# A graph network in two parts on one core: another order of the node blocks in the second part, and two pairs of steps swapped

## The chip, the cores and the metric

The kernel runs on one core of one Trainium2 chip. The metric is the device time of one execution, in microseconds (us). Every run gives one such time; what is compared is the median of several runs.

## The reference

There are 6250 nodes with 64 features each and 200,000 directed edges, sorted by their destination. A first network (one attention layer with a gate) and a normalisation come first. Then comes the second network, in which the change lies: three layers of attention over the edges with eight heads, each followed by a gate and a small two-layer network. `dst` and `src` are an edge's destination and source node, `edge_attr` is the same in all three layers.

```python
edge_attr = _mlp(_ln(edge_embed, eng, enb), eW1, eb1, eW2, eb2)
for l in range(L):                                   # L = 3
    h = _ln(x, n1g[l], n1b[l])
    xi, xj = (h[dst], h[src])
    q = (xi @ Wq[l] + bq[l]).reshape(-1, H, HD)      # H = 8 heads of HD = 8
    kn, vn = ...                                     # xj @ Wkn[l], xj @ Wvn[l]
    ke, ve = ...                                     # edge_attr @ Wke[l], edge_attr @ Wve[l]
    alpha = (q * (kn + ke)).sum(-1) / scale
    amax = jax.ops.segment_max(alpha, dst, num_segments=n)
    ex = jnp.exp(alpha - amax[dst])
    den = jax.ops.segment_sum(ex, dst, num_segments=n)
    alpha = ex / (den[dst] + 1e-16)
    msg = ((vn + ve) * alpha[..., None]).reshape(-1, D)
    agg = jax.ops.segment_sum(msg, dst, num_segments=n)
    gate = jax.nn.sigmoid(agg @ Wih[l] + bih[l] + h @ Whh[l] + bhh[l])
    upd = agg + gate * (h @ Wself[l] + bself[l] - agg)
    x = x + upd @ Wout[l] + bout[l]
    h2 = _ln(x, n2g[l], n2b[l])
    x = x + _mlp(h2, mW1[l], mb1[l], mW2[l], mb2[l])
```

## The kernel before

**Blocks.** The nodes are sorted by their number of edges and cut into 49 blocks of 128, one node to a partition. Block 0 holds the nodes with the most edges, block 48 those with the fewest. A block has SL[b] columns: column k holds the k-th edge of each of its nodes, so that a block's attention is a softmax along a row of columns. The first NW = 20 columns ("o") hold only edges with sources in certain blocks: column k those from blocks k, k + 20 and k + 40. The rest hold the other edges: the "a" columns have a gathered row each, and the "z" columns use such a row a second time. SL goes from 56 for block 0 down to 32 for block 48.

**Where the source rows come from.** At the end of a layer (or of the first network) each node's key and value products are stored in DRAM as a row of a table (`tab`), split into three bfloat16 parts. There are two such tables, for even and odd layers. A layer reads its table in two ways. First, the whole table is copied once into SBUF (`ftb`, seven copies of seven blocks, `refill`, L1274); the "o" columns take their rows from it by multiplying with 0/1 matrices `ohl`, which are loaded for each block (L1246). Second, for the other columns POOL issues indirect DMAs, one for each "gather" of 128 rows (L1254): NT[b] of them for block b, from 30 for block 0 to 7 for block 48, 859 in all. Gathers of a block are cut into chunks of at most CL = 12 (`cuts`); a chunk fills one buffer of the tile `g1`, and there are four such buffers (the pool `l_g`). The first four chunks are asked for when a layer starts (`start`); after that, using up a chunk asks for the one that is four further on in the order of blocks (`gather`, called in the main loop). The chunks of block 0 are 10, 10, 10, those of block 1 are 10, 10, 7, of blocks 2 and 3 they are 10, 10, 5, of block 4 12 and 12; blocks with 13 to 24 gathers have two chunks and those with up to 12 have one.

**A block's life.** The loop of L1479 counts i, and in iteration i block b = LORDER[i] has its columns summed, while the blocks b1, b2, b3 and b4 of the four iterations before it go through their later stages. In program order an iteration does the following.

- The softmax of b1 (`soft`), the norm of b3's new x (`updated`), and the weighted sum over b1's values (`values`), all on VectorE with the exponential on ScalarE; then the small loads of the next block (`begin`).
- The query of b (L1504). Then, group of columns by group of columns, `sums`: TensorE adds into a PSUM tile `b_pk` the products of the edge features (L1324), and either the rows picked from `ftb` (L1344) or the gathered rows (L1331); ScalarE copies keys and values out of it (L1348). After a part of the columns VectorE makes the scores (`scores`, L1355 and L1356). `b_pk` has two buffers.
- Between the groups six steps are called, spread evenly over them (the list `steps`, L1512 to L1515). They hold the work of b2, b3 and b4.

The functions that the steps call are these:

- `turned`: b2's weighted sum `b_ag` is transposed on TensorE (L571, in the helper `flip`) and copied out by ScalarE (L574).
- `gate` and `gated`: three products on TensorE (L1405 to L1407), a tanh on ScalarE (L1409), and four VectorE operations (from L1414 on).
- `update`: b2's output product; `updated`, in the next iteration, adds it to x (L1425) and normalises.
- `turned2`: b3's normalised x, `b_h2`, is transposed in the same helper (L571) and copied out with scale and shift (L576). The profile writes names without their last digits, so it shows as `b_h`.
- `hidden` and `close`: the small network of b3 (L1436, L1443 to L1445), the sum into x (L1446), the store of x, and the start of `prepare`, which makes the next layer's table row: a norm, a transposition (L601), a product (L613) with copies, and further parts of the split. b4 takes these parts one at a time through `then` and `more`.

**What sets the order.** The code of this network is under a manual schedule: each engine runs its instructions in program order. SyncE's queue carries the loads of edge features, of the 0/1 matrices, the small loads and the stores; POOL's queue carries the gathers, and in the last layer the output rows. The transpositions and the products of `gate`, `update`, `hidden`, `close` and `prepare` share the PSUM tile `p_pm`, which has two buffers (the pool `l_m`). After the 49 blocks a layer has four more iterations in which no block is summed; in them the steps of the last blocks run back to back.

**The order of blocks.** Before, it was

```python
48, 47, 1, 46, 0, 45, 2, 44, 3, 43, 4, 42, 5, 41, ..., 21, 25, 22, 24, 23
```

Block 48 has to come before block 0: the last block has unused rows that carry a part of the edges of block 0's nodes, and `values` joins them there.

Of the kernel before, what the change touches and what calls it, by code (L numbers as in the profile page):

```python
# [47 lines left out]
LB = NB - 1  # L48
# [1 line left out]
SPARE = P - LN  # L50
ORDER = (1, LB, 0) + tuple(range(2, LB))

LORDER = (LB, LB - 1) + tuple(b for i in range(24) for b in ((1, 0, *range(2, 24))[i], LB - 2 - i)) [:-1]
CAPE = tuple(c + c % 2 for c in CAPS)
FIRST = tuple(sum(CAPS[:b]) for b in range(NB + 1))
SLOTS = FIRST[NB]
# [54 lines left out]
def cuts(c, last=False, most=CH):  # L111

    if last:
        k = (c - 6) // 2 * 2
        return [(0, k), (k, c)]
    n = -(-c // most)
    w = 2 * -(-c // (2 * n))
    return [(k, min(k + w, c)) for k in range(0, c, w)]
# [3 lines left out]
def gnn_resnorm(ctx: ExitStack, tc: tile.TileContext, ins: dict, out: bass.AP):  # L122
# [33 lines left out]
    with tc.tile_pool(name="hd", bufs=1) as hd, tc.tile_pool(name="hd2", bufs=2) as hd2, \  # L156
# [271 lines left out]
        nc.vector.tensor_scalar(flag, vio[:, 2:3], 0.0, None, ALU.not_equal)  # L428

    passes(tc, ins, out, meta_d, t0_d, own_d, ident, row_f, ones, norm_c, st_i, id_i, off, end, has, hash_, rdeg, flag)  # L430
    away = nc.values_load(flag[0:1, 0:1], min_val=0, max_val=1)
    with tc.If(away > 0):
# [4 lines left out]
def passes(ctx, tc, ins, out, meta_d, t0_d, own_d, ident, row_f, ones, norm_c, st_i, id_i, off, end, has, hash_, rdeg,  # L437
# [143 lines left out]
    def flush():  # L581
        while stores:
            stores.pop(0)()
# [49 lines left out]
    with tc.tile_pool(name="e_g", bufs=4) as gp, tc.tile_pool(name="e_x", bufs=2) as xp, \  # L633
# [475 lines left out]
        for i in range(NB + 4):  # L1109
# [46 lines left out]
            for s in range(STEPS):  # L1156

                b = bs[3]
# [48 lines left out]
    with tc.tile_pool(name="l1", bufs=1) as fp, tc.tile_pool(name="l_g", bufs=4) as gp, \  # L1207
# [8 lines left out]
        todo = {}  # L1216
        for b in LORDER:
            tn, lc = NT[b], LCAPS[b]
            todo[b] = [(b, 0, 12, "o", 0), (b, 12, NW, "o", 0)]
            for t0, t1 in cuts(tn, b == LORDER[-1], CL):  # L1220
                todo[b].append((b, NW + t0, NW + t1, "a", t0))
                o0, o1 = max(tn, 2 * tn - t1), min(lc, 2 * tn - t0)
                if o0 < o1:
                    todo[b].append((b, NW + o0, NW + o1, "z", t0))
        loads = [(l, *t[:3]) for l in range(3) for b in LORDER for t in todo[b]]
        gathers = [(b, t0, t1) for b in LORDER for t0, t1 in cuts(NT[b], b == LORDER[-1], CL)]
        ohq = [(l, b, w0) for l in range(3) for b in LORDER for w0 in list(range(0, NW, 4)) + [NW]]
        eas, gs, ohs, ms, wanted_ = {}, {}, {}, {}, []

        def load():  # L1230
            if loads:
                l, b, k0, k1 = loads.pop(0)
                e0, e1 = k0 // 2, (k1 + 1) // 2
                eas[l, b, k0] = ep.tile([P, 8, P], F32, name="eal")
                nc.sync.dma_start(eas[l, b, k0][:, : e1 - e0, :], ea_d[b][:, e0:e1, :])

        def load_oh():
            if ohq:
                l, b, w0 = ohq.pop(0)
                if w0 == NW:  # L1240
                    oh = ohs[l, b, w0] = op.tile([P, 2, P], BF, name="oh2", bufs=3)
                    nc.sync.dma_start(oh, oh_d[b][:, NU * P :].rearrange("p (u n) -> p u n", n=P))
                    return
                n, u0 = 4 * most(w0), unit(w0, 0)
                oh = ohs[l, b, w0] = op.tile([P, 12, P], BF, name="ohl")
                nc.sync.dma_start(oh[:, :n, :], oh_d[b][:, u0 * P : (u0 + n) * P].rearrange("p (u n) -> p u n", n=P))  # L1246

        def gather(l):
            if wanted_:
                b, t0, t1 = wanted_.pop(0)  # L1250
                g = gs[l, b, t0] = gp.tile([P, CL, WT], F32, name="g1")
                for t in range(t0, t1):
                    f = TFIRST[b] + t
                    nc.gpsimd.indirect_dma_start(  # L1254
                        out=g[:, t - t0, :], out_offset=None, in_=tabs[l % 2][:],
                        in_offset=bass.IndirectOffsetOnAxis(ap=idx[:, f : f + 1], axis=0))

        def begin(l, b):
            hv = wk.tile([D + 1, P], F32, name="hv", bufs=5)
            nc.sync.dma_start(hv, ht_d[l % 2][b][:])  # L1260
            xb = wk.tile([P, D], F32, name="b_x", bufs=6)
            nc.sync.dma_start(xb, (x1_d if l == 0 else x2_d)[b][:])
            xv = None
            if l == 2:
                xv = wk.tile([P, D], F32, name="xv", bufs=6)
                nc.sync.dma_start(xv, x1_d[b][:])
            ms[b] = dict(hv=hv, xb=xb, xv=xv)
# [13 lines left out]

        begin(0, LORDER[0])
        for _ in range(5):
# [7 lines left out]
        i = 0  # L1291
        while i < NB:
# [4 lines left out]
            i = j  # L1297
# [15 lines left out]
        for l in range(3):  # L1313
# [39 lines left out]
            def scores(m, k0, k1):  # L1353
                k = m["k"][:, : k1 - k0]
                nc.vector.tensor_tensor(k, k, m["q"].unsqueeze(1).to_broadcast([P, k1 - k0, D]), ALU.mult)  # L1355
                nc.vector.tensor_reduce(m["al"][:, :, k0:k1].rearrange("p h k -> p k h"), k.rearrange("p k (h d) -> p k h d", h=H),  # L1356
                                        AX.X, ALU.add)
# [113 lines left out]
            def put():  # L1471
                while last:
                    b, n, y = last.pop(0)
                    nc.gpsimd.indirect_dma_start(
                        out=out[:], out_offset=bass.IndirectOffsetOnAxis(ap=id_i[:n, b : b + 1], axis=0),
                        in_=y[:n, 1, :], in_offset=None)

            last = []
            for i in range(NB + 4):  # L1479
                b, b1, b2, b3, b4 = [LORDER[i - k] if 0 <= i - k < NB else None for k in range(5)]  # L1480

                def do(b, *fs):
                    if b is not None:
                        for f in fs:
                            f(b, ms[b])

                do(b1, soft)
                do(b3, updated)
                do(b1, values)
                if i + 1 < NB:  # L1490
                    begin(l, LORDER[i + 1])
                elif i == NB and l < 2:
                    begin(l + 1, LORDER[0])
                if l < 2 and i == 1:
                    fresh = weights(l + 1)
                    nxt = next(fresh)
                if l < 2 and i == 2:
                    next(fresh, None)
                groups = []
                if b is not None:  # L1500
                    m, c = ms[b], SL[b]
                    qe = aps.tile([P, 512], F32, name="b_qe")
                    m["q"], m["ex"] = qe[:, :D], qe[:, D : D + c * H].rearrange("p (h k) -> p h k", h=H)
                    nc.tensor.matmul(m["q"], m["hv"], w["wc"][:, :D], start=True, stop=True)  # L1504
                    m["al"] = wk.tile([P, H, c], F32, name="b_al")
                    m["v"] = wk.tile([P, D, MS], F32, name="b_v")
                    for part in todo[b]:
                        k0, k1 = part[1:3]
                        n = -(-(k1 - k0) // 8)
                        n = 2 * -(-(k1 - k0) // (2 * n))  # L1510
                        groups += [(part, u, min(u + n, k1)) for u in range(k0, k1, n)]
                steps = [lambda: (do(b4, then), do(b2, turned)),  # L1512
                         lambda: (do(b3, turned2), do(b2, gate, gated)), lambda: do(b4, more, then),
                         lambda: (do(b3, hidden), do(b4, more)), lambda: (do(b3, close), do(b4, then)),
                         lambda: (do(b2, update), do(b4, more))]  # L1515
                done = 0
                for j, (part, u0, u1) in enumerate(groups):
                    k0, k1, kind = part[1:4]
                    if u0 == k0:
                        m["k"] = wk.tile([P, 16, D], F32, name="b_k", bufs=3)  # L1520
                    sums(m, part, u0, u1)
                    if u1 == k1:
                        scores(m, k0, k1)
                        load()

                        if kind != "o" and (j + 1 == len(groups) or groups[j + 1][0][4] != part[4]):
                            gather(l)
                    if kind == "o":
                        load_oh()
                        if u1 == k1:  # L1530
                            load_oh()
                        if u1 == NW:
                            load_oh()
                    while done < len(steps) and done < len(steps) * (j + 1) // len(groups):
                        steps[done]()
                        done += 1
                for f in steps[done:]:
                    f()
                flush()
                put()  # L1540
                if b4 is not None:
                    stored.add(b4)
                if l < 2 and b is None:
                    refill(l + 1, stored, left)
# [695 lines left out]
```

## Time and profile before

Five runs took 10798.19 to 10823.06 us, with a median of 10804.39. The profiled execution took 10803.97 us, and its span, from the first recorded instruction to the last, is 10802.2 us.

| stretch of the span | us | PE busy | DVE busy | ACT busy | POOL busy | PE clock |
|---|---|---|---|---|---|---|
| up to the second network, 0 to 4798.6 | 4798.6 | 2511.4 | 2402.7 | 1463.4 | 1725.9 | 0.71 |
| first layer, 4798.6 to 6764.2 | 1965.6 | 1442.8 | 1043.0 | 534.7 | 795.0 | 0.78 |
| second layer, 6764.2 to 8754.6 | 1990.4 | 1458.7 | 1043.8 | 535.3 | 829.4 | 0.77 |
| third layer and the end, 8754.6 to 10802.2 | 2047.6 | 1448.9 | 1164.2 | 498.2 | 877.1 | 0.76 |
| whole span | 10802.2 | 6861.8 | 5653.6 | 3031.6 | 4227.4 | 0.74 |

PE is TensorE, DVE is VectorE, ACT is ScalarE, POOL is GpSimd and SP is SyncE; PEld is the loading of weights into TensorE. Busy means that an instruction's own time lies there; issuing a DMA from SyncE is not counted, while an indirect DMA on POOL is. The PE clock is the share of full speed that was granted. A row of the profile's groups reads: line, engine, operation, output tile and input tiles, number of instructions, then after the bar the busy time and the mean of one in ns, then the idle time of the engine just ahead of them and what ended most of it. A row of the timeline reads: start, duration, engine, line, operation, number of instructions, and in brackets the idle time before it with what released it; "issue" means that the engine waited for nothing that the profile can show.

In a layer TensorE has the most busy time of the four engines, some 1450 of 1966 to 2048 us. Its two largest groups in the second network are the picking of rows from `ftb` (L1344, 1930.1 us in three layers) and the products of the edge features (L1324, 1414.0 us).

### The profile page before, as it was taken

The numbers are of one execution on the slowest core, as the hardware profiler recorded it, in microseconds if no ns is written. First come the engines' busy times: TensorE is split into PE (matmuls) and PEld (weight loads), VectorE is DVE, ScalarE is ACT, GpSimd is POOL, SyncE is SP. The second block draws the span as 40 slices with busy tenths as digits, with TensorE's granted clock in tenths as the row PEclk, the third lists the DMA queues.
The fourth block names the chain that finished last, engine by engine and source line by source line (L and its number), as shares of the span: only waits on it lengthen the run. The fifth ranks groups of instructions, "written<-read, shape, count | busy, mean of one in ns | idle before, by whom it ended". The sixth has DMA issues, their size and how long they took to land.

```text
span 10802.2 us, 162686 instructions
## 1 busy us (share of the span) xinstructions
PE 6861.8 (64%) x61936; PEld 4733.5 (44%) x61936; DVE 5653.6 (52%) x14987; ACT 3031.6 (28%) x6298; POOL 4227.4 (39%) x4450
## 2 busy tenths in 40 slices
PE   2535455555555555666777777567777766777776
PEld 1212222222222223335556666456566645665665
DVE  5535455544445555534555555355555544656556
ACT  1323233322333333332222223222222222222222
POOL 5343433333333333324444443444444434444443
PEclk6667777766766677777777777777777777777777
DMA  4333333333333333344444444444444444444443
GB/s 101 98 89 93 99 98 98 90 94 95 95 89 92 91 92 89 95 110 130 131 126 133 134 134 133 123 126 131 131 135 132 132 127 114 128 127 124 130 129 92
DMA packets 1089117, 1218.64 MB, mean 113 GB/s; under 512 B 654756, under 2 KB 810041, under 8 KB 1081295
## 3 DMA queue, kind: packets, MB, share of 16 engines
q1 hardware_dynamic: 626639, 719.43, 22.6%
q0 software_dynamic: 186576, 417.85, 15.3%
q10 hardware_dynamic: 275120, 70.87, 3.2%
q8 instruction: 498, 8.16, 0.3%
q14 instruction: 284, 2.33, 0.1%
HBM read 968.74 MB, written 238.86 MB: 112 GB/s over the span
## 4 chain that ended last, share of the span: by engine, by line
PE 53%; another core or an unknown queue 19%; issue 18%; ACT 5%; DVE 3%; DMA 1%; POOL 0%; SPq 0%; ACTq 0%; POOLq 0%; DVEq 0%
PE b_pk L1344 18%; PE b_pk L1324 12%; PE f_ph L996 6%; PE b_pk L1331 4%; PE f_tr L959 4%; PE f_pe L978 3%; ACT f_hid L1000 1%; ACT f_sq L759 1%; ACT ea L982 1%; PE p_pm L1436 1%; ACT s_bc L841 1%; PE p_pm L838 1%; PE p_pm L1445 1%; ACT f_xt L963 1%
## 5 line engine op out<-in xcount | busy, mean ns | idle before, releaser
L1254 POOL DMA_INDIRECT g<-tab,fidx x2577 | 2487.2, 965 | 3546.9 <-PE b_pk L1331 1721.6
L740 POOL DMA_INDIRECT g<-ft_d,si x1596 | 1522.9, 954 | 2795.1 <-PE e_pt L1059 2322.5
L1344 PE MATMUL b_pk<-ftb,ohl 128*128 128x128 bf16 x21609 | 1930.1, 262 | 732.3 <-issue 684.0
L1344 PEld LDWEIGHTS <-ohl 128*128 128x128 bf16 x21609 | 1715.9, 121 | 971.4 <-issue 929.1
L1324 PE MATMUL b_pk<-fwkv,eal 64*128 64x128 f32 x12240 | 1414.0, 315 | 710.5 <-issue 660.1
L1355 DVE TENSOR_TENSOR b_k<-b_k,b_qe 128x768 f32<-128x768 f32 (+8 forms) x729 | 519.9, 713 | 2425.4 <-ACT b_k L1348 1834.7
L1324 PEld LDWEIGHTS b_pk<-fwkv,eal 64*128 64x128 f32 x12240 | 1038.5, 203 | 990.4 <-issue 881.7
L1348 ACT COPY b_k<-b_pk 128x384 f32<-128x384 f32 (+2 forms) x927 | 445.5, 481 | 3547.0 <-remote 1462.4
L978 PE MATMUL f_pe<-f_hid,fw 128*64 128x448 f32 (+4 forms) x2400 | 754.2, 650 | 1071.2 <-issue 716.8
L996 PE MATMUL f_ph<-f_xt,fw 64*128 64x448 f32 (+4 forms) x2400 | 821.4, 700 | 555.1 <-ACT f_xt L963 482.3
L963 ACT ACTIVATE f_xt<-f_tr,feg 128x336 f32<-128x336 f32 (+11 forms) x392 | 247.3, 631 | 2253.2 <-remote 1891.2
L978 PEld LDWEIGHTS f_pe<-f_hid,fw 128*64 128x64 f32 x2400 | 153.0, 152 | 1541.2 <-issue 1049.8
L1348 ACT COPY b_v<-b_pk 128x384 f32<-128x384 f32 (+2 forms) x927 | 822.5, 887 | 0.0
L1000 ACT ACTIVATE f_hid<-f_ph,fb 128x448 f32<-128x448 f32 (+4 forms) x1200 | 694.6, 624 | 448.1 <-PE f_ph L996 303.8
L959 PE MATMUL f_tr<-f_mv,f_xs 128*64 128x42 f32 (+11 forms) x12544 | 577.9, 255 | 346.7 <-issue 344.1
L946 DVE TENSOR_TENSOR f_mv<-s_tt,e_fac 128x672 f32<-128x672 f32 (+11 forms) x392 | 333.4, 851 | 874.7 <-remote 718.8
L959 PEld LDWEIGHTS f_tr<-f_mv,f_xs 128*64 128x64 f32 x12544 | 528.9, 167 | 456.4 <-issue 430.2
L996 PEld LDWEIGHTS f_ph<-f_xt,fw 64*128 64x128 f32 x2400 | 267.4, 223 | 912.6 <-ACT f_xt L963 614.7
L1356 DVE TENSOR_REDUCE b_al<-b_k 128x96 f32<-128x768 f32 (+8 forms) x729 | 520.7, 714 | 25.1
L1331 PE MATMUL b_pk<-g,oh 128*128 128x384 bf16 (+2 forms) x2682 | 496.8, 321 | 0.0
L1375 DVE TENSOR_REDUCE b_ag<-b_v 128x64 f32<-128x2560 f32 (+19 forms) x147 | 430.5, 2928 | 5.1
L1374 DVE TENSOR_TENSOR b_v<-b_v,b_qe 128x2560 f32<-128x2560 f32 (+19 forms) x147 | 429.1, 2919 | 0.0
(405 smaller groups left out, 7649.7 us busy)
## 6 DMA issues: line engine op xcount, KB each, us to landing
ohl<-oh_d SPq DMA_DIRECT2D x441, 384.0 KB
ohl<-oh_d SPq DMA_DIRECT2D x294, 256.0 KB
eal<-ea_d SPq DMA_DIRECT2D x189, 384.0 KB
eal<-ea_d SPq DMA_DIRECT2D x249, 256.0 KB
oh_d<-s_oh SPq DMA_DIRECT2D x147, 384.0 KB
g<-tab,fidx POOLq DMA_INDIRECT x2577
eal<-ea_d SPq DMA_DIRECT2D x117, 320.0 KB
ea_d<-ea ACTq DMA_DIRECT2D x154, 224.0 KB
```

The costliest lines, as they stand in the source:

```text
L740: nc.gpsimd.indirect_dma_start(out=g[:, k - k0, :], out_offset=None, in_=t0_d[:], in_offset=bass.IndirectOffsetOnAxis(ap=got[b]["si"][:, k ...
L959: nc.tensor.matmul(pv[r * D : (r + 1) * D, j], xss[(4 * ORDER.index(b) + 4 * j0 // D) % 4][:, (j0 + j) % (D // 4), :], mv[:, j, :, r::2], ...
L978: nc.tensor.matmul(pe[h * D : (h + 1) * D, :w], w2[:, s, :], hid[s][:, h, :w], start=(s == 0), stop=(s == 1))
L996: nc.tensor.matmul(ph[h][:, :w], w1[r, s * P : (s + 1) * P], xf[r, e0 * D : e1 * D], start=True, stop=True)
L1000: nc.scalar.activation(hid[s][:, h, :w], ph[h][:, :w], AF.Relu, bias=b1[:, s : s + 1])
L1254: nc.gpsimd.indirect_dma_start(out=g[:, t - t0, :], out_offset=None, in_=tabs[l % 2][:], in_offset=bass.IndirectOffsetOnAxis(ap=idx[:, f : ...
L1324: nc.tensor.matmul(pk[:, j % 2, j // 2, :], ea[r, e, :], w["wkv"][r], start=(j < 2), stop=False)
L1331: nc.tensor.matmul(pk[:, h, :c, :], ohs[l, b, NW][:, 0, :], rows_[:, slice(t, t + 2 * c - 1, 2), i, :], start=False, stop=(i == 2))
L1344: nc.tensor.matmul(pk[:, h, j, :], o, rows[:, i, :], start=False, stop=(j == c - 1 and q == len(us) - 1 and i == 2))
L1348: nc.scalar.copy(to.rearrange("p (j h) d -> p h j d", h=2), pk[:, :, : n // 2, d0 : d0 + D])
L1355: nc.vector.tensor_tensor(k, k, m["q"].unsqueeze(1).to_broadcast([P, k1 - k0, D]), ALU.mult)
L1356: nc.vector.tensor_reduce(m["al"][:, :, k0:k1].rearrange("p h k -> p k h"), k.rearrange("p k (h d) -> p k h d", h=H), AX.X, ALU.add)
```

## The change

Two things change, in the constants and in the main loop of the second network. No function is added, and the six steps hold the same calls.

```diff
-LORDER = (LB, LB - 1) + tuple(b for i in range(24) for b in ((1, 0, *range(2, 24))[i], LB - 2 - i)) [:-1]
+LORDER = (LB, LB - 1, LB - 2, LB - 3) + tuple(b for i in range(23) for b in ((1, 0, *range(2, 23))[i], LB - 4 - i))[:-1]
...
-                steps = [lambda: (do(b4, then), do(b2, turned)),
-                         lambda: (do(b3, turned2), do(b2, gate, gated)), lambda: do(b4, more, then),
+                steps = [lambda: (do(b2, turned), do(b4, then)),
+                         lambda: (do(b2, gate, gated), do(b3, turned2)), lambda: do(b4, more, then),
                          lambda: (do(b3, hidden), do(b4, more)), lambda: (do(b3, close), do(b4, then)),
                          lambda: (do(b2, update), do(b4, more))]
```

The first makes the order of blocks

```python
48, 47, 46, 45, 1, 44, 0, 43, 2, 42, 3, 41, 4, 40, ..., 20, 24, 21, 23, 22
```

so a layer starts with four blocks of few edges instead of two, then goes on with pairs of a large and a small block as before; a large block now stands beside one that is two places further on in the small ones. The last block is 22 instead of 23; both have 17 gathers.

The second puts, in the first step, the transposition of b2's attention ahead of b4's pending part of the next table, and in the second step b2's gate ahead of the transposition of b3's normalised x.

## The prediction

> **What bounds the kernel now.** I read the page first. The second network (lines 1207 to 1545) fills the last 6,000 us of the span, in three layers, and TensorE works through its blocks in program order. The largest idle sum in front of its matmuls is laid to "issue", that is, to no semaphore at all. POOL's largest group is the row gather of L1254.
>
> ```profile
> span 10802.2 us, 162686 instructions
> L1254 POOL DMA_INDIRECT g<-tab,fidx x2577 | 2487.2, 965 | 3546.9 <-PE b_pk L1331 1721.6
> L1344 PE MATMUL b_pk<-ftb,ohl 128*128 128x128 bf16 x21609 | 1930.1, 262 | 732.3 <-issue 684.0
> ```
>
> 2577 gathers in three layers are 859 a layer, as the sum of NT says. Next the timeline of the second layer's first block (its columns: start, us, engine and instruction, count, idle before).
>
> ```profile
> 6801.54 0.95 POOL L1254 DMA_INDIRECT g<-tab,fidx  x1 [0.30 <-issue]
> 6802.51 0.27 PE L1344 MATMUL b_pk<-ftb,ohl 128*128 128x128 bf16 x1 [2.53 <-issue]
> 6802.80 0.95 POOL L1254 DMA_INDIRECT g<-tab,fidx  x1 [0.30 <-issue]
> 6805.31 0.26 PE L1344 MATMUL b_pk<-ftb,ohl 128*128 128x128 bf16 x1 [2.53 <-issue]
> ```
>
> A gather goes out every 1.25 us (0.95 + 0.30), and beside such a run TensorE gets one matmul off in 2.8 us, though nothing it needs is missing. After the run the same line does 48 matmuls in 2.85 us (at 6962.87). So a run of gathers is itself the cost. I therefore read the busy time by stretch, one stretch for each run of the second layer (us, PE, PEld, DVE, ACT, POOL busy with counts, clock, DMA share, GB/s).
>
> ```profile
> 6768.85:6814.05 45.20, 11.58 (x96) 7.99 (x95) 0.00 (x0) 1.24 (x2) 34.29 (x36) 0.58 0.40 108
> 6829.76:6838.55 8.79, 5.79 (x77) 4.63 (x77) 7.15 (x8) 1.34 (x5) 6.73 (x7) 0.94 0.38 107
> 6853.61:6866.15 12.54, 4.88 (x55) 4.44 (x55) 11.02 (x26) 1.12 (x3) 9.70 (x10) 0.73 0.70 220
> 6940.60:6954.40 13.80, 6.15 (x70) 4.70 (x69) 12.15 (x33) 1.12 (x3) 10.48 (x11) 0.72 0.40 104
> 7065.40:7090.50 25.10, 10.87 (x83) 8.15 (x84) 4.46 (x7) 4.87 (x15) 19.04 (x20) 0.65 0.38 106
> 7148.40:7178.50 30.10, 12.65 (x88) 8.59 (x88) 4.46 (x7) 4.87 (x15) 22.84 (x24) 0.66 0.38 104
> 7182.80:7192.90 10.10, 6.50 (x66) 5.29 (x65) 9.41 (x20) 1.21 (x3) 7.94 (x8) 0.84 0.49 130
> 7211.80:7218.10 6.30, 4.20 (x56) 3.46 (x56) 5.63 (x24) 1.34 (x5) 4.86 (x5) 1.00 0.46 116
> 7234.90:7250.00 15.10, 9.22 (x75) 7.03 (x72) 6.26 (x16) 3.67 (x8) 11.07 (x12) 0.79 0.35 96
> ```
>
> Length less PE busy is TensorE's idle time in a run: 36 gathers 33.6, 7: 3.0, 10: 7.7, 11: 7.7, 20: 14.2, 24: 17.5, 8: 3.6, 5: 2.1, 12: 5.9 us. Two more stretches of the same view, which follow a run of 20: 10 gathers from 6911.29 on, 3.6 us, and 5 from 7000.85 on, 0.7 us. The price is not linear: a short run is almost free, a long one costs nearly its length. The data themselves are early: of the second layer, block 48's gathers are out at 6777 and its first L1331 starts at 6826. Gathers late for a large block, which the old order could be suspected of, are not seen.
>
> **The change, part by part: the order.** No instruction is added or removed; each block keeps its work, its 96 gather chunks a layer and its loads. What moves is which chunk is fetched when. Four buffers of g1 hold four chunks, so using up chunk j releases the gathers of chunk j+4, and the two first chunks of a block with three run on without a break, the third after one of about 4 us (25.1 us, a break, then 5 or 10, in the stretches above). With LORDER and NT I write out the runs from the start of a layer until the blocks 1, 0, 2, 3, 4, 5 and 48 to 41 are fetched, and strike what both orders have. Left before: 36, 11 (block 45), 20 and 5 (block 3), 24 and 8 (block 4 and part of 42), 5, and block 41's 8 and 5. Left after: 37, 10, 8, 15 and 10, 5 and 8, 17 and 12. Both are 122 gathers in nine runs.
>
> Before: 33.6 + 7.7 + 14.2 + 0.7 + 17.5 + 3.6 + 2.1 + 3.6 + 2.1 = 85.1 us. After, the 37 is 33.6 + 1.3 = 34.9. The single 10 follows a small block, as the 7.7 did (its other row is 3.6). For the others the trace has no run: 8 behind a small block lies between 7 (3.0) and 10 (7.7), I take 4.6; 15 and 17 lie between 12 (5.9) and 20 (14.2), straight between them 9.0 and 11.1, with 5.9 as lower end for both and 14.2 and 17.5 (the run of 24) as upper. Sum: 34.9 + 7.7 + 4.6 + 9.0 + 3.6 + 2.1 + 3.6 + 11.1 + 5.9 = 82.5 us. That is 2.6 us less a layer. The ends are 68.5 and 97.2 us, so 16.6 less or 12.1 more. In the first layer the run of 36 lies ahead of the first block's start at 4798.6, in the end of the first network, so its 1.3 us cost nothing there: 3.9 less. Three layers: 2.6 + 2.6 + 3.9 = 9.1 us less. Past these blocks the pairs of large and small go on as before, only shifted by two, with the same run lengths, and the last five blocks hold 17 to 19 gathers each in both orders. Block 48's spill still goes out two or more blocks ahead of block 0, and 7 tables refill in the same two groups, since the blocks 21 to 27 are the last ones stored in both; these cost nothing because their place stays.
>
> One rule of the Trainium skill speaks against a gain here. "TensorE: Matmul & The Clock Gate", section "Architectural detail", gives TensorE a queue of 64 instructions. If 64 queued entries alone covered a run, each run would cost its length less one constant; 122 gathers in nine runs would then cost the same in both orders, and the sum would be 9.1 us higher. The rows above bend (10 for 7.7, 7 for 3.0, 20 for 14.2), so I keep them.
>
> **The steps.** In step 1 of the list (L1512) the transposition of b_ag (L571) goes ahead of the next table's (L601); in step 2 the gate's products (L1405 to L1407), its tanh (L1409) and its four VectorE operations go ahead of the transposition of b_h. Within a running block this moves instructions of 0.3 to 0.7 us past each other on TensorE and ScalarE; SP's and POOL's queues hold nothing of them. From 7200 to 8690 TensorE waits at L601 and L571 15.3 us in all, nearly all of it "issue": the matmuls of the block hide the rest. I take 0, with 1.5 us a layer (its waits for VectorE there) as the gain's end. What is queued behind the gate now is b_h's transposition, which the hidden layer needs two steps later. At the end of a layer there is no cover:
>
> ```profile
> 6741.76 0.42 PE L601 MATMUL p_pm<-fident,p_hn 128*64 128x128 f32 x1 [2.12 <-DVE p_hn L552]
> 6742.08 0.42 PE L571 MATMUL p_pm<-fident,b_ag 128*64 128x128 f32 x1
> 6744.64 0.40 PE L571 MATMUL p_pm<-fident,b_h 128*64 128x128 f32 x1 [2.14 <-DVE b_h L552]
> 6744.97 0.69 PE L1405 MATMUL p_pm<-hv,fwc 65*64 65x128 f32 x2
> 6747.03 0.28 DVE L1414 SCALAR_TENSOR_TENSOR b_gt<-b_at,p_pm 64x128 f32<-64x128 f32 x1 [2.54 <-ACT b_gt L1409]
> 6747.77 1.22 PE L1436 MATMUL p_pm<-b_h2t,fm 64*128 64x128 f32 x4 [0.36 <-ACT p_kf L614]
> 6750.61 0.22 DVE L1446 TENSOR_TENSOR b_x<-b_x,p_pm 128x64 f32<-128x64 f32 x1 [2.23 <-PE p_pm L1421]
> ```
>
> The gate stands from 6742.5 behind a transposition that waits for VectorE until 6744.6. Put ahead of it, its products fit into that wait (1.7 us of them). L613 (0.8 us) can then start at 6745.1 and L1436 at 6745.9 instead of 6747.8, and L1446, from which the rest of the chain runs on VectorE to the last table and the next layer's gathers, comes 1.8 us earlier. The iteration before is bound by VectorE without a gap, so nothing is won there; the two after it have no gate. The end of the program has the same place without L613: L1436 at 10772.96 could follow the transposition of 10770.97 at 10771.9, 1.1 us less. Sum 1.8 + 1.8 + 1.1 = 4.7 us, with 0 as the other end.
>
> **Sum.** The profiled execution took 10803.97 us, of which the span is 10802.2; the median shown is 10804.39, 0.4 us away. 10804.0 - 9.1 - 4.7 = 10790.2; I say 10791.
>
> **Rivals.** Slower: runs flow together. Its place is block 3 and block 2 in the new order, whose third chunk follows a first run of only 17 or 15 gathers; if its buffer is free by then, 29 and 25 gathers go without a break. By the 24's 17.5 us and 1.25 for each further one these cost 23.8 and 18.8 instead of 17.0 and 12.6: 13 us a layer more, 10791 + 39 = 10830. It decides from the point where TensorE gives the third buffer free within the first run. For it: one such joined run of 21, of 12 and 9, from 5643.8 to 5669.9 left TensorE 9.2 of 26.1 us busy, so it took 17. Against it: in all four blocks with three chunks the break came after runs of 20 and of 24 alike, since TensorE, starved, gives the buffer free only when the run ends.
> Faster beyond what can be told from no change: the split runs cost what the cheap rows say (15 and 17 near 5.9, the 10 at 3.6). Half way to that end is 9.6 us a layer less: 10804 - 30 - 5 = 10769. For it: 5 and 8 in sequence cost 2.1 and 3.6. Against it: every run above 10 gathers behind a large block cost at least 5.9.
> The swap makes a stall: in the third layer the gate now takes the p_pm buffer that L1425 empties, so TensorE would wait there for VectorE. The longest wait at these transpositions now is 6.8 us (for L602, once in the layer); once more in each layer is 20 us, 10811. Against it: b_h, for which TensorE waited at that very place before, is made after L1425.
>
> **How the numbers follow.** Forecast (10783 to 10803 as its own range) 0.52; faster rival 0.31; joined runs 0.13; stall 0.04. 0.2% is 21.6 us, about what a measurement of this kernel can tell from no change: below 10782.8 is faster, above 10826.0 slower. The forecast and most of the stall lie within; the faster rival gives 0.31 and a part of the forecast's tail 0.02: 0.33; slower, the joined runs and a part of the stall, 0.14; same 0.53. The cheap ends of all terms together give 10804 - 3 x 16.6 - 4.7 = 10749, so the faster rival spreads from 10783 to 10749; the range reaches into it to 10757 and to 10828, close to the joined runs, and leaves a tenth on each side.
>
> **What would show it.** In the profile after: runs of 37, 10, 10, 7, 12, 20, 10 gathers at each layer's start; 15 and 17 with 8 to 12 us of TensorE idle; the gate's L1405 ahead of b_h at a layer's end, and L1446 there some 2 us sooner after the transposition. The forecast is wrong if the runs of block 3 join, or if a run's cost does not depend on its length as the rows say, or if idle time outside the runs moves.

## The result and the profile after

The changed kernel takes 10828.34 us (median of 25 runs), the kernel before 10815.36 us (46 runs); the ratio is 1.0015, with a 95% interval of 1.0008 to 1.0021. That is some 9 to 23 us slower, which counts as no change by the 0.2% named above, but it is clear of zero and on the other side than forecast, and the median lies 0.3 us outside the range (10828.0). Of the 37 us between the 10791 of the forecast and this median, 11 lie in the kernel before: it took 10815.36 us here, and 10804 us when the forecast was made from it. The profiled execution of the changed kernel took 10827.36 us.

The page of the changed kernel, the same three lines as before:

```profile
span 10825.6 us, 162695 instructions
L1254 POOL DMA_INDIRECT g<-tab,fidx x2577 | 2486.1, 965 | 3577.6 <-PE b_pk L1331 1757.4
L1344 PE MATMUL b_pk<-ftb,ohl 128*128 128x128 bf16 x21609 | 1936.7, 261 | 795.2 <-issue 756.2
```

Work and counts are the same. The idle time in front of L1344 is 795.2 instead of 732.3 us, and the part of it that is laid to "issue" is 756.2 instead of 684.0. That isn't yet the loss: with the new order and the steps of before (an experiment below, which takes as long as the kernel before) these sums are 828.4 and 790.0. By stretches, worked out from the two traces: from the first query of a layer (L1504) to its last sum into `b_pk`, the three layers took 1924.9, 1949.5 and 1987.8 us before and 1935.9, 1958.4 and 2003.0 after, that is 11.0, 8.9 and 15.2 more. From that last sum to the next layer's first query, or to the end, they took 40.7, 40.7 and 59.9 before and 38.6, 38.6 and 58.8 after, 5.3 less in all. So the ends gave what was forecast for them, and the running blocks lost. How much they lost, one execution of each can't say: a version below whose blocks run as before took 1933.4, 1945.2 and 2003.3 us.

Where the blocks lose shows in the timeline of one block each, after a run of gathers is over, in the second layer. First the kernel before, around the second step:

```profile
7626.43 1.00 PE L1344 MATMUL b_pk<-ftb,ohl 128*128 128x128 bf16 x15
7627.26 0.27 PE L571 MATMUL p_pm<-fident,b_h 128*64 128x128 f32 x1
7627.47 0.43 PE L1405 MATMUL p_pm<-hv,fwc 65*64 65x128 f32 x2
...
7628.41 0.94 PE L1324 MATMUL b_pk<-fwkv,eal 64*128 64x128 f32 x12
```

and the changed kernel at the same place:

```profile
7627.11 1.00 PE L1344 MATMUL b_pk<-ftb,ohl 128*128 128x128 bf16 x15
7628.04 0.43 PE L1405 MATMUL p_pm<-hv,fwc 65*64 65x128 f32 x2
...
7628.98 0.30 PE L571 MATMUL p_pm<-fident,b_h 128*64 128x128 f32 x1
7629.21 0.94 PE L1324 MATMUL b_pk<-fwkv,eal 64*128 64x128 f32 x12
```

No instruction of these rows waits for anything in either. But before, the transposition starts 0.17 us ahead of the (modelled) end of the bfloat16 group, and the block goes on with L1324 0.98 us after that end (7628.41 against 7627.43). After, the gate's first product starts only 0.07 us ahead of it, the transposition behind the products takes 0.30 instead of 0.27, and L1324 follows 1.10 us after the end of the group. The same place moves by 0.12 us in block after block: from the start of the last `b_pk` product ahead of the gate's group to the start of the next one behind it is 1.20 us in the median of 138 blocks before, and 1.32 after. 138 x 0.12 = 16.6 us.

At a layer's end the gate goes ahead as forecast (timeline of the changed kernel at the end of the first layer):

```profile
6746.39 0.39 PE L601 MATMUL p_pm<-fident,p_hn 128*64 128x128 f32 x1 [1.86 <-DVE p_hn L552]
6746.71 0.69 PE L1405 MATMUL p_pm<-hv,fwc 65*64 65x128 f32 x2
...
6749.18 0.39 PE L571 MATMUL p_pm<-fident,b_h 128*64 128x128 f32 x1 [0.74 <-DVE b_h L552]
6753.09 0.22 DVE L1446 TENSOR_TENSOR b_x<-b_x,p_pm 128x64 f32<-128x64 f32 x1 [1.80 <-PE p_pm L1421]
```

The products now fill part of TensorE's wait for b_h, which is down from 2.14 to 0.74 us, and L1446 comes 6.70 us after L601's start, where it came after 8.85.

The experiments met two conditions (the expectations speak of kinds of chip, but chip 2 gave both), a quick one in which the kernel before takes about 6660 us at a granted clock of 0.90 to 0.91, and a slow one like that of the profiles above, 10730 to 10815 us at 0.74, and each run is compared only with runs of the kernel before measured beside it.

### The profile page after: what moved, and what is told of

Read it like the earlier page. It is cut to its first block, busy times and chain, and to the rows that moved or that the text cites. A ratio compares the mean times of both kernels' runs of the same rounds, so it can differ in the third digit from the quotient of the medians.

```text
span 10825.6 us, 162695 instructions
## 1 busy us (share of the span) xinstructions
PE 6867.1 (63%) x61936; PEld 4737.1 (44%) x61936; DVE 5648.9 (52%) x14987; ACT 3047.4 (28%) x6298; POOL 4224.6 (39%) x4450
## 5 line engine op out<-in xcount | busy, mean ns | idle before, releaser
L1344 PE MATMUL b_pk<-ftb,ohl 128*128 128x128 bf16 x21609 | 1936.7, 261 | 795.2 <-issue 756.2
L1344 PEld LDWEIGHTS <-ohl 128*128 128x128 bf16 x21609 | 1713.1, 121 | 1042.7 <-issue 1009.0
L1324 PE MATMUL b_pk<-fwkv,eal 64*128 64x128 f32 x12240 | 1405.2, 315 | 686.7 <-issue 616.9
L1355 DVE TENSOR_TENSOR b_k<-b_k,b_qe 128x768 f32<-128x768 f32 (+7 forms) x729 | 520.0, 713 | 2487.6 <-ACT b_k L1348 1981.4
L1348 ACT COPY b_k<-b_pk 128x384 f32<-128x384 f32 (+2 forms) x927 | 445.6, 481 | 3622.1 <-remote 1597.8
L1324 PEld LDWEIGHTS b_pk<-fwkv,eal 64*128 64x128 f32 x12240 | 1045.0, 204 | 937.4 <-issue 793.0
L1348 ACT COPY b_v<-b_pk 128x384 f32<-128x384 f32 (+2 forms) x927 | 822.3, 887 | 0.0
L1356 DVE TENSOR_REDUCE b_al<-b_k 128x96 f32<-128x768 f32 (+7 forms) x729 | 520.6, 714 | 25.1
```

What stands on the lines that cost most here:

```text
L1324: nc.tensor.matmul(pk[:, j % 2, j // 2, :], ea[r, e, :], w["wkv"][r], start=(j < 2), stop=False)
L1344: nc.tensor.matmul(pk[:, h, j, :], o, rows[:, i, :], start=False, stop=(j == c - 1 and q == len(us) - 1 and i == 2))
L1348: nc.scalar.copy(to.rearrange("p (j h) d -> p h j d", h=2), pk[:, :, : n // 2, d0 : d0 + D])
```

## The experiments

In the expectations R is the theory that the loss lies in how the gather runs fall after the new order, and S that it lies in the swapped steps. P is S with the place named, once the first traces had shown it: the 0.12 us of the transposition behind the float32 products. Q and O are P's rivals: by Q the gate's place as such is dear, by O the loss needs the order and the steps together. They are told by subject, not in order of time.

### The two parts alone

The order alone (`LORDER` of the diff, old steps) and the steps alone (steps of the diff, old `LORDER`), first under the quick condition:

> Only the new order of blocks, with the old order inside the two steps. Theory R (the loss lies in how the gather runs fall after the new order: a 20 and a 24 for blocks 2 and 3, where 15 and 17 were forecast): the loss is all here, and the 5 us that the steps save at the ends of the layers are missing, so 1.0017 to 1.0025, some 18 to 27 us slower than before. Theory S (the swapped steps cost TensorE a little in each of the 147 block iterations, the order gains as forecast): 0.9985 to 1.0000, 0 to 16 us faster. In the profile, R: TensorE's idle time in gather runs is 10 to 15 us above before's over three layers; S: the later blocks (from the 17th of a layer on) take the time they took before.

> Only the two swapped steps, with the old order of blocks. Theory R: 0.9990 to 1.0000, that is 0 to 10 us faster, of which 5 us at the ends of the three layers (40.7, 40.7 and 59.9 us become some 38.6, 38.6 and 58.8), and nothing within the running blocks. Theory S: 1.0015 to 1.0030, with the loss of 0.2 to 0.3 us for each of 147 blocks spread over the layers.

Measured: the order 1.0001 (0.9991 to 1.0011), the steps 1.0013 (1.0003 to 1.0024). So under this condition the loss is in the steps. The changed kernel and the kernel before under the same condition:

> The changed kernel itself once more, because the four runs before this were on a chip on which the kernel before takes 6664 us instead of 10815. If this chip is of that kind: theory R says that the order's loss is gone with the starving of TensorE in gather runs, which those traces don't show, so 0.9985 to 1.0005 with the steps' gain alone; theory S says 1.0010 to 1.0025, as for the swapped steps alone there. If it is of the slower kind: 1.0015 again.

> The kernel before itself, for a profile on the same chip beside the changed one: on a chip of the quicker kind 6650 to 6680 us, with the blocks of the first two layers bound by POOL's gathers in one run of some 700; on a chip of the slower kind 10780 to 10850 us with runs of 5 to 36 as in the profile read for the prediction.

The changed kernel measured 1.0008 (0.9998 to 1.0018), which alone decides nothing; the kernel before gave 6678.37 us with a profile. Its traces are so regular there that the price can be read block by block: in the first two layers a block of the middle takes 23.2 or 21.4 us in the kernel before and 23.3 or 21.5 with the swapped steps, and the two layers (first query to last sum) take 1134.5 and 1112.9 us before, 1140.7 and 1121.3 with the steps alone. The group of the gate is again 1.20 against 1.32 us. The blocks grow by what the group grows, which speaks for P and leaves little to Q. The order alone also lengthens these layers, to 1139.8 and 1120.3, at least in part by another cause: POOL issues gathers without a break there, and TensorE waits for rows in some late blocks (16 times, 8.5 us). Both together give 1140.0 and 1118.3, not the sum. The third layer isn't that regular: it takes 1245.8 us before, 1242.0 with the steps and 1235.6 with the order, so over three layers the order alone is 2.5 us longer in these traces, which agrees with its 1.0001.

Both parts once more, later, under the slow condition:

> The swapped steps alone, in the old order, once more, to have them on the other kind of chip too. Theory P: 138 x 0.12 = 16.6 us within the blocks, less 5 us at the layers' ends: on a chip of the slower kind 1.0005 to 1.0020 (12 us are 1.0011), on one of the quicker kind 1.0013 again. Rival O (the loss there is of the order and the steps together, since the new order alone was not run there): 0.9990 to 1.0003.

> The new order alone once more. Theory P: no loss, 0.9993 to 1.0008 on either kind of chip. Rival O: 1.0010 or more on the slower kind.

Measured 1.0002 (0.9988 to 1.0015) for the steps and 0.9999 (0.9987 to 1.0012) for the order, with 10730.07 us for the kernel before. For the order that speaks against O, which had 1.0010 or more. For the steps, their 12 us (16.6 - 5) are inside the interval, but so is nothing, and the ratio itself is one that O had named: this run doesn't decide. The traces of the two profiled executions tell the parts apart better: the gate's group is 1.32 us with the steps and 1.20 with the order.

### Which pair of steps

```diff
-                         lambda: (do(b3, turned2), do(b2, gate, gated)), lambda: do(b4, more, then),
+                         lambda: (do(b2, gate, gated), do(b3, turned2)), lambda: do(b4, more, then),
```

> The kernel before with only the second pair of steps swapped (gate ahead of b_h's transposition). Theory P: the whole price of the swapped steps is here: the group takes 1.32 instead of 1.20 us in all three layers, layers 1 and 2 are 5 to 6 us longer each, 1.0005 to 1.0020 in all. If the first pair is the dear one: 1.0000, and 1.32 us is then made up elsewhere.

Measured (quick condition) 1.0012 (1.0003 to 1.0022); the group takes 1.32 us, and the layers 1141.2 and 1118.4. The whole price is in the second pair; the first pair takes 0.37 us in either order, from the start of the product ahead of it to the start of the one behind.

### Taking the price away by another place: a miss

```diff
-                         lambda: (do(b2, gate, gated), do(b3, turned2)), lambda: do(b4, more, then),
+                         lambda: do(b2, gate, gated), lambda: (do(b3, turned2), do(b4, more, then)),
```

> The changed kernel (new order, gate first), with b_h's transposition taken from behind the gate's float32 products and put at the head of the third step, behind bfloat16 products of the block. Theory P (the swap's price is 0.12 us in each of 138 blocks, because the transposition no longer starts beside the last bfloat16 products): the gate's group falls from 1.32 to 1.09 us, the third step's grows by 0.11, so each block gets back 0.12 us; layers 1 and 2 shrink by 5 us each against the changed kernel where TensorE binds them, and the whole is 0.9990 to 1.0003 of the kernel before. Rival Q (the price is the place of the gate, whose tanh and VectorE work come at another time): the groups change as said, but the layers keep the changed kernel's length, 1.0005 to 1.0020.

Two more of the kind, on the kernel before: L601 moved from the first step to the head of the second, and that together with the gate ahead and b_h's transposition in the third step.

> The kernel before with the next table's transposition (L601) moved from the first step to the head of the second, ahead of b_h's. In the traces the first step's pair takes 0.37 us in blocks of many edges but 1.0 to 2.8 us in some 14 to 17 of the blocks of few edges, where p_hn is late. If that wait is on the path: 14 x 0.9 = 13 us a layer in layers 1 and 2, so 0.9960 to 0.9985. If POOL's gathers or VectorE bind those blocks as well, the wait is only moved: 0.9990 to 1.0010.

> Old order, and in the steps: b_ag's transposition alone first; then the next table's transposition and the gate; then b_h's transposition with the table's product. Theory P and the late p_hn together: the gain of the run with the later table, and the gate goes ahead without the price, with its 5 us at the layers' ends: 0.9955 to 0.9980; it would be the quickest of all. If only P holds: 0.9985 to 1.0000.

Measured (quick condition): 1.0299 (1.0285 to 1.0313), 1.0271 (1.0255 to 1.0287) and 1.0277 (1.0263 to 1.0292). All three expectations failed. In the first, the gate's group did fall to 1.09 us, but a new wait stands behind the moved instruction. So it couldn't tell P from Q. The waits of TensorE, first of the kernel with L601 later, then of the one with b_h's transposition in the third step (columns: what waited and for what, us in total, times, longest):

```profile
PE p_pm L1405 <- ACT fht L602: 138.3, 90, 1.7
```

```profile
PE p_pm L613 <- ACT b_h2t L576: 134.7, 84, 1.8
```

There are two buffers of `p_pm`. In each of these versions an instruction needs a third while both are held: by L601's and b_h's transpositions in the one, by the gate's products, which VectorE has yet to read, and b_h's transposition in the other. The copy that frees the next one (L602 or L576) stands behind ScalarE's large copies of the block (L1348). So the third taker waits some 1.5 us with everything behind it, 90 times in the one and 84 in the other; the version with both changes has the wait of L613 too (137.7 us, 85 times). The first two layers together are 169 to 206 us longer than before, so these waits are the larger part of the loss and not all of it. The changed kernel doesn't have this wait: its second step takes two buffers, as before. Whether the late p_hn of L601 costs anything in itself isn't answered by these runs.

### Taking the price away where it arises

The steps as before while a block is being summed, and the gate first only in the iterations at a layer's end, with the old order and with the new one:

```diff
+                first = (lambda: (do(b3, turned2), do(b2, gate, gated))) if b is not None else \
+                    (lambda: (do(b2, gate, gated), do(b3, turned2)))
```

> Old order; the steps as before while a block is being summed (b_h's transposition ahead of the gate), and the gate first only in the four iterations at a layer's end, where no block is left. Theory P: within the blocks nothing is paid (group of the gate 1.20 us), layers 1 and 2 keep the kernel before's length (on a chip of the quicker kind 1134.5 and 1112.9 us from the first query to the last sum, within 1.5), and the ends give 2.1, 2.1 and 1.1 us: 0.9985 to 1.0003 of before, the best of the versions. Rival Q (the gate's place as such is dear): the ends give nothing either, 1.0000.

> The new order with the same steps. Theory P: the changed kernel less 0.12 us in each of 138 blocks. On a chip of the quicker kind the layers take what the order alone gave (1139.8 and 1120.3 us), since POOL's gathers bind there, 0.9985 to 1.0010; on a chip of the slower kind 1.0015 less 0.0015, 0.9993 to 1.0007 of before, and the order itself is then worth nothing there.

Measured (slow condition): 0.9998 (0.9989 to 1.0006) with the old order, and 1.0001 (0.9992 to 1.0009) with the new one. The second is the changed kernel without the price: in place of 1.0015 (1.0008 to 1.0021) it has 1.0001, with intervals that just touch; the group is back at 1.20 us, and the ends take 39.0, 39.1 and 59.1 us. TensorE's busy time over the second network says the same (stretches of the kernel before, of the changed kernel and of this one, with the columns of the prediction's stretches):

```profile
4798.60:10802.20 6003.60, 4350.41 (x41868) 3492.10 (x41868) 3250.95 (x7491) 1568.23 (x3563) 2501.50 (x2590) 0.77 0.45 128
4792.20:10825.60 6033.40, 4364.27 (x41868) 3502.30 (x41868) 3245.87 (x7491) 1584.41 (x3563) 2499.55 (x2589) 0.77 0.45 127
4796.90:10809.40 6012.50, 4347.89 (x41868) 3486.19 (x41868) 3252.09 (x7491) 1569.41 (x3563) 2507.49 (x2589) 0.77 0.45 128
```

The same matmuls take 4364.3 us with the swapped steps, 4350.4 and 4347.9 without, some 14 to 16 us less. The first version, meant as the best of these versions, can't be told from the kernel before: 5 us of 10807 are 0.05%.

### Are the gather runs a cost at all

The prediction summed the order's effect from the idle time of TensorE by the length of a run. To test that price by itself, the runs were broken up: after each group of columns POOL copies one value which ScalarE has just written for that group, and then issues at most three of the gathers that are due (or six). Only what is left of a chunk that a block is about to read goes out without this limit.

```diff
+        def pump(n, after=None):
+            if pend and after is not None:
+                nc.gpsimd.tensor_copy(tick, after)
+            for _ in range(min(n, len(pend))):
+                _, _, to, f, l = pend.pop(0)
+                nc.gpsimd.indirect_dma_start(
...
+                    if kind != "o":
+                        pump(sum(p[:2] == (b, part[4]) for p in pend))
                     sums(m, part, u0, u1)
+                    pump(3, m["v"][:, 0, u0 : u0 + 1])
```

Under the quick condition, with the old order and with the changed kernel:

> The kernel before, with the same gathers issued at most three at a time: after each group of columns POOL copies one value that ScalarE has just written for this group, and then issues up to three of the gathers that are due. Theory run length (a run starves TensorE only when it goes on for more than about 5 us, as the rows 5: 0.7 to 2.1 us against 36: 33.6 say): runs of three cost 0 to 0.7 us, so 390 us of idle time in a layer's runs fall to 0 to 200, and the kernel takes 10100 to 10400 us. Theory share (each gather costs TensorE about 0.45 us wherever it stands, 390 us over 859): within 50 us of before, 10750 to 10850. Slower than 10850 if POOL's waits make the gathers late for L1331.

> The changed kernel with the same pacing of gathers as in the run beside it. Theory R: the difference of the two orders lies in how runs join; with no run above three it is gone, so this is 0 to 15 us faster than the paced kernel with the old order and steps (the 5 us of the layers' ends, and an early start of a layer that is no longer starved). Theory S, or any loss of the order that has nothing to do with runs: it stays some 16 us slower than that one.

Measured 1.0154 (1.0135 to 1.0173) and 1.0174 (1.0152 to 1.0196). The two intervals overlap, so R and S aren't told apart by them. There is little to gain, because TensorE is hardly starved there. In the kernel before under that condition, a stretch of 800 us in which POOL never stops (columns: us, busy time and count of PE, PEld, DVE, ACT and POOL, clock, DMA share, GB/s):

```profile
3300.00:4100.00 800.00, 789.27 (x10299) 666.02 (x10300) 747.97 (x1691) 388.78 (x909) 607.35 (x633) 1.00 0.77 233
```

633 gathers at 1.26 us fill the 800 us, and TensorE is busy for 789 of them. Where the pacing's 1.5% comes from isn't shown; late rows it isn't, since TensorE waits for gathered rows 1.1 us in the paced kernel of the old order and 1.0 us in the kernel before. Then under the slow condition:

> The kernel before with at most three gathers at a time, as before on the quicker kind, where it took 1.0154. On a chip of the slower kind, if a run's cost to TensorE goes by its length as the prediction summed it: runs of three at 0 to 0.7 us, 10100 to 10500 us. If each gather costs the same wherever it stands: 10750 to 11000, with the pace's own cost. On the quicker kind 1.0154 again.

> The same with at most six gathers after each group of columns. Slower kind, if length decides: runs of five and six cost 0.7 to 2.1 us, so between the kernel before and the one with three, 10300 to 10650; if the gather decides, 10750 to 10950. Quicker kind: POOL is held less, 1.000 to 1.012.

Measured: 9982.85 us with at most three, 0.9323 (0.9297 to 0.9348) of the kernel before beside it, by far the quickest version under this condition and below the range that was expected; and 10921.6 us with at most six, 1.0191 (1.0169 to 1.0213), a miss. The timeline of POOL in the first of them:

```profile
7246.03 1.02 POOL L1262 DMA_INDIRECT g<-tab,fidx  x1 [0.48 <-issue]
7247.36 0.96 POOL L1262 DMA_INDIRECT g<-tab,fidx  x1 [0.31 <-issue]
7248.62 0.96 POOL L1262 DMA_INDIRECT g<-tab,fidx  x1 [0.30 <-issue]
7252.14 0.18 POOL L1259 COPY tick<-b_v 128x1 f32<-128x1 f32 x1 [2.56 <-ACT b_v L1357]
```

Three gathers, then a pause until ScalarE has written the next group. Worked out from the traces, the mean time within a run in which no matmul ran (a break of more than 0.7 us ends a run; not every length is listed):

| gathers in a run | kernel before: runs, us | at most three: runs, us | at most six: runs, us |
|---|---|---|---|
| 3 | none | 228, 0.05 | 6, 1.39 |
| 5 | 15, 1.04 | 10, 0.46 | 15, 0.59 |
| 6 | 12, 1.87 | 97, 1.98 | 25, 1.51 |
| 8 | 75, 2.79 | 9, 3.25 | 75, 4.07 |
| 9 | 23, 3.34 | 89, 4.06 | 19, 4.07 |
| 10 | 66, 4.21 | 3, 4.92 | 61, 5.53 |
| 12 | 29, 6.25 | 8, 5.98 | 31, 7.10 |
| 36 | 3, 33.12 | none | none |
| all, three layers | 1176 | 712 | 1327 |

So the price by length is real under this condition, and runs of three cost next to nothing. With at most three, the runs of six and nine are two and three portions end to end, where the next group was written before the portion was out; they hold 553 of the 712 us.

The idle time in runs isn't all that was saved. Stretches of the second network, of the new order alone (0.9999, measured at the same time) and of the kernel with at most three, with the columns of before:

```profile
4790.60:10724.30 5933.70, 4318.02 (x41868) 3457.71 (x41868) 3252.84 (x7491) 1568.41 (x3563) 2500.97 (x2589) 0.77 0.45 130
4731.40:9982.50 5251.10, 4055.96 (x41868) 3231.13 (x41868) 3237.47 (x7491) 1564.04 (x3563) 2708.40 (x3507) 0.82 0.50 147
```

Of the 683 us between them, 403 are idle time in runs (1113.5 and 710.5 us), and 262 are busy time: the same 41868 matmuls take 4056 instead of 4318 us, at a granted clock of 0.82 instead of 0.77, and both ratios are 0.94. A further 59 us lie ahead of the second network, where the edit changes nothing; why isn't shown. With at most six, the runs did not become short: those of 8, 10 and 12 are there as often as before, two portions end to end, and each costs about 1 us more. Why each costs more wasn't tried.

## Why the prediction was wrong

- **The step that failed: "I take 0" for the steps within a running block.** It moved "instructions of 0.3 to 0.7 us past each other", and their price was bounded by TensorE's waits at L601 and L571 alone. In the running block shown, nothing waits at that place before or after; what changed is how closely neighbours overlap. A transposition between the block's bfloat16 products and the gate's float32 products adds 0.11 us to the group (1.09 without it, 1.20 with it), behind the float32 products 0.23 (1.32). The trace of before could have warned of it by the start-to-start times at that place, though not by the durations, since a later start and a longer overlap leave every duration nearly alone; what the other place costs it doesn't show. The Trainium skill's page "TensorE: Matmul & The Clock Gate", section "Part 4: PE-mode transpose", gives about 275 ns for a 128x128 bfloat16 transposition in one kernel's context. The rows here, float32 and of 64 columns, have 0.27 and 0.30 us, close to that, and the group's 0.11 and 0.23 us show that the duration isn't what a transposition adds.
- **The order: forecast 9.1 us less, measured about nothing** (0.9999 under the slow condition; with the old place of the gate in the blocks 1.0001 for the new order beside 0.9998 for the old). The times alone leave room for 9 us, as 0.9999 has an interval from 0.9987 to 1.0012. The runs themselves say more: over the first 334 gathers of each layer, TensorE's idle time in the runs is 188.8, 193.2 and 184.9 us before and 192.1, 191.9 and 183.8 after, no gain. The term that was off is how chunks join for blocks 2, 3 and 4. Forecast were runs of 15 and 10, and of 17 and 12. In the third layer they came; in the first two, the chunk of 5 went out alone and the next two chunks joined, to 20 and to 24:

```profile
7142.30:7167.20 24.90, 9.76 (x61) 6.96 (x62) 17.50 (x38) 3.17 (x10) 19.06 (x20) 0.50 0.41 111
7225.50:7255.40 29.90, 8.74 (x62) 5.99 (x62) 17.64 (x38) 3.17 (x10) 22.86 (x24) 0.54 0.40 106
9135.60:9154.30 18.70, 11.52 (x89) 7.88 (x87) 4.35 (x7) 4.46 (x12) 14.31 (x15) 0.78 0.43 113
9220.80:9242.00 21.20, 10.92 (x86) 7.83 (x84) 4.26 (x6) 4.43 (x12) 16.22 (x17) 0.75 0.41 109
```

  These are stretches of the changed kernel, with the columns of the stretches above: the run of 20 leaves TensorE idle for 15.1 us and that of 24 for 21.2, the 15 and the 17 of the third layer for 7.2 and about 10.3. The forecast had 9.0 and 11.1 for these two, and 17.5 for a 24. So the prices were near and the list of runs was not. How chunks join isn't fixed by the order alone: when the order was run by itself under the slow condition, the 15 and the 10 came in all three layers, and the same sum over three layers was 533.9 us, beside 546.3 for the old order measured at the same time. That would be 12 us of gain in the runs, and the interval of that run can neither show nor exclude it.
- **The ends: right, by the mechanism that was named.** Forecast 4.7 us, measured 5.3 (2.1, 2.1 and 1.1). The 1.1 of the last end rests on single executions, in which that end varies by more than 1 us from run to run of the same steps.
- **The rivals.** Runs of 29 and 25 did not come; chunks joined, but in another way and at a smaller price. In the changed kernel the split runs were there in the third layer only, at 7.2 and 10.3 us and not near the 5.9 of the faster rival. The stall's wait did come, at the end of the third layer: L1405 waits for L1425 there, once, for 8.1 us. It cost nothing, for the reason that was put against it: before, the transposition of b_h waited 10.5 us for VectorE at that place, and the end as a whole became shorter.
- **The queue of 64 instructions**, which the prediction took from the skill's page "TensorE: Matmul & The Clock Gate", section "Architectural detail", and weighed against the rows. If the queue alone covered a run, a run's cost would be its length less one constant. By the kernel before in the table, length less cost is 5.0 us for runs of five, 8.2 for ten and 11.9 for 36 (lengths 6.1, 12.4 and 45.0 us), so it isn't constant, and keeping the rows was right. A queue that is still fed slowly during a run isn't excluded: in the prediction's stretches, a run of 12 has 75 matmuls and the run of 36 has 96.

Sum with the measured terms: 16.6 in the blocks, 5.3 less at the ends and nothing for the order are 11 us more, inside the 9 to 23 of the result, where the forecast had 13.8 less. The two terms that failed, 16.6 put at 0 and 9.1 put as a gain, make up the difference. That each block passes its whole 0.12 us on is read from the quick condition, where the blocks of the first two layers grow by 0.1 us each; under the slow one single executions vary by more than that sum, and whether anything else adds to the loss there stays open.

## What to carry to other kernels

When instructions are moved past each other on the engine that sets a block's time, compare the time from the last instruction ahead of the group to the first one behind it: a swap that added no wait there cost 0.12 us here, 138 times. A step that is moved takes its PSUM buffer with it; count how many of a pool of two are still waiting for ScalarE at the new place before anything else. And ahead of a re-ordering of work that shifts costs about, test whether the cost itself can be taken away: three gathers at a time brought 6.8% under the slow condition, where the order brought nothing that could be measured.

## What the runs showed of the hardware

- Under the slow condition matmuls crawl as soon as a run of gathers lasts more than some 5 us: runs of three (3.5 us) leave TensorE idle for 0.05 us, runs of ten (12.4 us) for 4.2, the run of 36 (45.0 us) for 33.1. Under the quick condition TensorE is busy 789 of 800 us beside gathers without a break, at a granted clock of 1.00 in that stretch. The number and the mean duration of the gathers are the same (2577, 965 and 961 ns). What makes the difference between the conditions isn't known.
- A change can be worth 7% under one and cost 1.5% under the other (at most three gathers: 0.9323 and 1.0154).
- With at most three gathers at a time the granted clock over the second network was 0.82 instead of 0.77, and the same matmuls were 6% shorter: breaking up the runs saved busy time as well as idle time.
